# Pacing the modulation rows of a fused adaLN block, with the low-rank loads moved behind them and another scheduling model

## The chip, the cores and the metric

The kernel runs on one core of a Trainium2 chip. The metric is the device time of one execution in microseconds (us); lower is better. Five engines work side by side, each with its own in-order instruction queue: TensorE (PE) for matrix products, with its weight loads shown apart as PEld; VectorE (DVE); ScalarE (ACT); GpSimd (POOL); and SyncE (SP), which here issues nearly all DMAs.

## What is computed

One transformer-like block on x of shape (4, 1024, 2048) in float32. Six modulation vectors per batch come from one product with a 100 MB weight; a long convolution (an S4 kernel of 2048 taps) runs along the last axis; then comes a 2048 x 2048 linear layer with a low-rank update from 16 experts.

```python
mod = (_silu(L0_c) @ L0_wmod).reshape(L0_c.shape[0], 6, 1, -1)
sa, ca, ga, sb, cb, gb = (mod[:, 0], mod[:, 1], mod[:, 2], mod[:, 3], mod[:, 4], mod[:, 5])
ga = (2 * (ga >= 0) - 1) * jnp.maximum(jnp.abs(ga), 0.25)
gb = (2 * (gb >= 0) - 1) * jnp.maximum(jnp.abs(gb), 0.25)
h = _layernorm(x, axis=-1) * (1 + ca) + sa
x = x + ga * _L0_attn_ref(h, ...)      # y = irfft(rfft(h) * rfft(K)); y + D * h
h = _layernorm(x, axis=-1) * (1 + cb) + sb
x = x + gb * _L0_ffn_ref(h, ...)       # h W^T + bias + sum_e w_e (h A_e^T) Bf_e^T
```

## The kernel before

The 4096 rows of x are 32 blocks of 128 rows. For each block the kernel takes the layer-norm statistics (`stats`, L535), normalizes on DVE (`normalize`, L552), transposes 16 pieces on PE (L573), scales and shifts them on ACT (L577) and splits them into high and low float16 halves (L587, L588). The convolution is then a Toeplitz product on PE (`conv_mm`, L608): 108 matmuls a block, in three families, 41,472 columns in all. `conv_post` stores the result and takes the second layer-norm's sums (L654). The linear layer follows for 16 units of 256 rows (`ffn_unit`, L744), 5376 matmuls in all.

**Modulation rows.** `wmod` is loaded in 96 pieces of 128 x 2048 floats (1 MiB each, `mod_load`, L312), 16 for each of the six vectors. I call a piece a row. A row costs PE four matmuls (`mod_mm`, L317). The 16 rows of a vector are a `section`, which accumulates in one PSUM bank and ends in a small chain that makes a column or a gate. Section 1 (scale ca) comes first, then 0 (shift sa), then 2 (gate ga), and 4, 3, 5 later. Rows land in two pools: `wmp` with three buffers and `wms` with two, which closes after section 0.

**Early blocks.** Blocks 0, 1 and 2 are multiplied before the gate is known (`early`). For 0 and 1 the shift is missing as well; `shift_conv` and `shift_add` put it in afterwards. In this kernel one row is taken at each of the 9 `tick` calls of an early block's `conv_mm`. When section 2 is done, `gate_tile` (L668, L669) spreads the gate over 128 partitions, `conv_late` (L644, L645) applies it to the three waiting blocks, `conv_post` finishes them, and only then are the buffers of x free for blocks 4, 5 and 6.

**The low-rank part.** `prep_lora` loads A (`la`, L427) and Bf (`lb`, L440), squares, scales and splits them on ACT and DVE (L432 to L457). `merge` then adds the low-rank product to W, in eight steps of 48 matmuls each (L481). These steps, with sections 4, 3 and 5 between them, are the generator `fill`, which is advanced by `step()` during the `conv_mm` of later blocks, from block `R0` = 3 on.

**Order.** The program text gives priorities; a list scheduler in the tile framework decides the order of instructions on every engine's queue from them and from a time model of its own. The order is fixed before the run. On the chip each queue is worked off strictly in that order. `tc.issue_after` and `tc.high_priority` bend the order around the S4 kernel's steps (`toe`, taken at the row numbers `KT`).

Of the kernel before, what the change touches and what calls it, by code (L numbers as in the profile page):

```python
# [24 lines left out]
P = 128  # L25
# [9 lines left out]
class Net:  # L35
# [197 lines left out]
    def toeplitz(self, pool):  # L233
        nc, v = self.nc, self.nc.vector
        rev = pool.tile([P, P], F32, tag="rev", name="rev")
        nc.gpsimd.memset(rev, 0.0)
        nc.gpsimd.affine_select(
            out=rev, in_=rev, compare_op=ALU.not_equal, fill=1.0, base=1 - P, pattern=[[1, P]], channel_multiplier=1
        )
        kk = pool.tile([P, 16], F32, tag="kk", name="kk")  # L240
        yield from self.s4(pool)
        v.tensor_copy(kk, self.kp)
        dt = pool.tile([1, 1], F32, tag="dt", name="dt")
        nc.scalar.dma_start(out=dt, in_=self.io["D"].unsqueeze(0))
        v.tensor_tensor(kk[0:1, 0:1], kk[0:1, 0:1], dt, ADD)
        m = pool.tile([P, 1], F32, tag="km", name="km")
        v.tensor_reduce(m, kk, AX.X, ALU.max, apply_absolute_value=True)
        s, self.kinv = self.pow2(self.cst, self.allmax(pool, m, 1, "km"), 1, "ks")
        v.tensor_scalar(kk, kk, s, None, MUL)
        kd = self.dram.tile([P + D], F32, tag="kd", name="kd")  # L250
        z = pool.tile([1, P], F32, tag="kz", name="kz")
        v.memset(z, 0.0)
        nc.scalar.dma_start(out=kd[0:P].unsqueeze(0), in_=z)
        nc.scalar.dma_start(out=kd[P:].rearrange("(a b) -> a b", b=16), in_=kk)

        kb = pool.tile([P, D], F32, tag="kb", name="kb")
        src = bass.AP(tensor=kd.tensor, offset=kd.offset + 1, ap=[[1, P], [1, D]])
        nc.scalar.dma_start(out=kb, in_=src)
        self.kb = kb
        yield  # L260
        for q in range(4):
            ps = self.acc.tile([P, 512], F32, tag="a", name="kbps")
            nc.tensor.matmul(ps, rev, kb[:, ds(512 * q, 512)], start=True, stop=True)
            (v.tensor_copy if q % 2 else nc.scalar.copy)(kb[:, ds(512 * q, 512)], ps)


        kv = kb.rearrange("p (m e t) -> p m e t", e=2, t=P)
        ev, od = kv[:, :, 0, :], kv[:, :, 1, :]
        self.kf = {}
        for f in (0, 2, 1):  # L270
            hi = self.kpool.tile([P, HC * P], F16, tag=f"kh{f}", name=f"kh{f}")
            lo = self.kpool.tile([P, HC * P], F16, tag=f"kl{f}", name=f"kl{f}")
            h3, l3 = (x.rearrange("p (m t) -> p m t", t=P) for x in (hi, lo))
            if f == 0:
                src = ev
            else:
                src = pool.tile([P, 2, 512], F32, tag="kdif", name="kdif")
                src = src.rearrange("p a (c t) -> p (a c) t", t=P)
                if f == 1:
                    v.tensor_scalar(src[:, 0:1], ev[:, 0:1], -1.0, None, MUL)  # L280
                    v.tensor_tensor(src[:, 1:], od[:, 0 : HC - 1], ev[:, 1:], SUB)
                else:
                    v.tensor_tensor(src, od, ev, SUB)
            v.tensor_copy(h3, src)
            v.tensor_tensor(l3, src, h3, SUB)  # L285
            self.kf[f] = hi, lo
        yield
# [21 lines left out]
    def mod_load(self, pool, sec, j):  # L309
        w = pool.tile([P, D], F32, tag="wm", name="wm")  # L310
        src = self.io["wmod"].rearrange("(p j) n -> p j n", j=16)
        self.nc.sync.dma_start(out=w, in_=src[:, j, ds(sec * D, D)])  # L312
        return w

    def mod_mm(self, w, j):
# [272 lines left out]
                v.tensor_tensor(lo[:, sl], src, hi[:, sl], SUB)  # L588
            yield

    def conv_mm(self, pl, hs, x, tick, early):
        nc, v = self.nc, self.nc.vector
        hc, hs = hs
        y = pl["y"].tile([P, D], F32, tag="y", name="y")
        yv = y.rearrange("p (j e t) -> p j e t", e=2, t=P)
        if not early:
            gv = self.gat.rearrange("p (j e t) -> p j e t", e=2, t=P)
        sums = pl["sm"].tile([P, 2], F32, tag="sums", name="sums")

        def family(ps, f, q, first):  # L600
            pf = ps.rearrange("p j t -> p (j t)")
            last = 4 * q + 3
            for i in range(last + 1):
                o = P * max(0, i - 4 * q)
                k0 = P * max(0, 4 * q - i)
                for x, z in ((0, 0), (0, 1), (1, 0)):
                    h = hs[x][:, i] if f == 0 else hc[x][:, 2 * i + 2 - f]
                    nc.tensor.matmul(  # L608
                        pf[:, o:512], h, self.kf[f][z][:, ds(k0, 512 - o)],
                        start=first, stop=(i == last and (x, z) == (1, 0)), skip_group_check=True,  # L610
                    )
                    first = False
                if i == 3 and q == 1:
                    tick()

        for q in range(2):
            jj = slice(4 * q, 4 * q + 4)
            pa = self.acc.tile([P, 4, P], F32, tag="a", name="ya")
            family(pa, 0, q, True)
            qs = pl["t"].tile([P, 4, P], F32, tag="qs", name="qs")  # L620
            nc.scalar.copy(qs, pa)  # L621
            tick()
            pb = self.acc.tile([P, 4, P], F32, tag="a", name="yb")
            family(pb, 2, q, True)
            v.tensor_tensor(yv[:, jj, 1, :], pb, qs, ADD)
            if not early:
                v.tensor_tensor(yv[:, jj, 1, :], yv[:, jj, 1, :], gv[:, jj, 1, :], MUL)
            tick()
            family(pa, 1, q, False)
            sl = ds(1024 * q, 1024)  # L630
            if early:
                nc.scalar.copy(yv[:, jj, 0, :], pa)
            else:
                v.tensor_tensor(yv[:, jj, 0, :], pa, gv[:, jj, 0, :], MUL)  # L634
                v.scalar_tensor_tensor(y[:, sl], y[:, sl], 1.0, x[:, sl], MUL, ADD, accum_out=sums[:, q : q + 1])  # L635
            tick()
        return y, sums
# [167 lines left out]
ACC, TPS = 5, 2  # L805
PLAN = ("PNSL", "NL", "NSL", "NTL", "SL", "SL", "SL", "SL", "FSL", "SSL")
LPLAN = ("LL", "LL", "LL", "LL", "L", "0", "")
R0 = 3
WM, WMS = 3, 2
EARLY = 3  # L810
X0 = 11
LEFT0 = 30
KT = (0, 5, 7, 11)


def STQ(nc):
# [8 lines left out]
def net(ctx: ExitStack, tc: tile.TileContext, io):  # L825
# [19 lines left out]
    def section(sec, pools):  # L845
        for q in range(16):
            if q == 0:
                k.mod_begin()
            k.mod_mm(k.mod_load(pools[q % len(pools)], sec, q), q)
            yield  # L850
        if sec == 0:
            k.sa = k.mod_column(msm, k.kpool, "sa", 0.0)
            k.hinv = k.fold_scale(msm, k.ca, k.sa, "fs1")
        elif sec == 1:
            k.ca = k.mod_column(msm, k.kpool, "ca", 1.0)
        elif sec == 2:
            k.gas, (k.gad,) = k.mod_gate(msm, "gad")
        elif sec == 4:
            k.cb = k.mod_column(msm, k.cst, "cb", 1.0)
        elif sec == 3:  # L860
            k.sb = k.mod_column(msm, k.cst, "sb", 0.0)
        else:
            _, k.gbd = k.mod_gate(msm, "gbd", io["bias"])
        yield

    def merges():
        k.prep_lora(pl["lora"], pl["mrg"])
        yield
        for c in range(HC):
            yield from k.merge(pl["lora"], pl["mrg"], c)  # L870
# [3 lines left out]
    def take(g, n):  # L874
        for _ in range(n):
            next(g, None)
# [12 lines left out]
    def prep(r, shift=True):  # L889
        return k.conv_prep(pl, r, xs[r], sts.pop(r), hs, shift)  # L890

    def load(r):
        xs[r] = k.conv_load(pl, r)

    def stats(r):
        sts[r] = k.stats(pl, xs[r], "1")
# [8 lines left out]
        n += 1  # L905
    k.early_scale(msm)
    load(1)
    sec = section(0, (wms, wmp))
    for r in range(2):
        stats(r)  # L910
        take(prep(r, False), 9)
    take(sec, 1)
    with tc.issue_after(k.last.ins), tc.high_priority():
        take(toe, 2)
    take(sec, 1)

    def row():
        take(sec, 1)

    for r in range(2):  # L920
        ys[r] = k.conv_mm(pl, hs.pop(r), xs[r], row, True)
        load(r + 2)
    take(sec, 17)
    k.shift_conv(msm)
    k.shift_add([ys[r][0] for r in range(2)])
    st.close()
# [48 lines left out]
        if r >= R0 and "w" not in pr and next(fill, 0) == 0:  # L975
            early()

    sec = section(2, (wmp,))
    for r in range(2, EARLY + 1):
        stats(r)  # L980
    take(prep(2), 9)
    ys[2] = k.conv_mm(pl, hs.pop(2), xs[2], row, True)
    nxt = prep(3)
    take(nxt, 9)
    take(sec, 17)
    k.gat = k.gate_tile(pl["g"], 0)
    ratio = k.kpool.tile([P, 1], F32, tag="rat", name="rat")
    nc.vector.tensor_tensor(ratio, k.einv, k.hs[:, 0:1], MUL)
# [5 lines left out]
    stats(EARLY + 1)  # L994
    nxt = prep(EARLY + 1)
    take(nxt, 1)
    post = None
    for r in range(EARLY, 32):
        if EARLY + 2 < r + 2 < 32:
# [129 lines left out]
```

## Time and profile before

| | us |
|---|---|
| runs, median of 3 | 2149.32 (2148.76 to 2154.0) |
| profiled execution | 2149.26 |
| its span, first to last instruction | 2147.5 |
| PE busy | 2085.0 (97%), 11144 matmuls |
| DVE busy | 1313.8 (61%) |
| ACT busy | 922.0 (43%) |
| DMA moved | 483.05 MB, 225 GB/s over the span |

Between span and run time lie 1.8 us. Busy PE is not PE at its peak: the profiler models the ends of matmuls, which overlap, so a lost nanosecond shows best as a longer distance between the starts of two neighbours. "Idle before" stands beside the instruction whose start ended the idle time, with what released it. PEclk is the granted TensorE clock as a share of full speed.

### The profile page before, as it was taken

What the parts mean: (1) busy time and instruction counts of PE and PEld (TensorE: products, weight loads), DVE (VectorE), ACT (ScalarE), POOL (GpSimd) and SP (SyncE); (2) the same over time, 40 slices, a digit from 0 to 9 for tenths busy, and PEclk for the clock granted to TensorE, in tenths of its full rate; (3) what the DMA queues carried; (4) which work ended last, traced back from release to release, by engine and by line L of the source; (5) the groups of instructions that cost most, each with busy time, mean ns of one, the idle gap of its engine ahead of it and who ended that gap; (6) DMA issues with size and microseconds to landing.
All of it is one profiled execution on the core that took longest, in us unless ns stands there. A gap on an engine that the chain in (4) does not pass through costs nothing.

```text
span 2147.5 us, 28491 instructions
## 1 busy us (share of the span) xinstructions
PE 2085.0 (97%) x11144; PEld 1028.0 (48%) x11144; DVE 1313.8 (61%) x2356; ACT 922.0 (43%) x1697; POOL 3.0 (0%) x13
## 2 busy tenths in 40 slices
PE   6998999999999999999999999999999999999999
PEld 2453445455455555554545545545444444444444
DVE  5636989988999998666566565565433323232323
ACT  1335757766677776655554454454200000000000
POOL 0000000000000000000000000000000000000000
PEclk7998999999999999999999999999999999999999
DMA  9878677767874463297465465564795545455542
GB/s 389 347 266 312 253 271 286 291 247 272 312 286 160 181 221 118 94 376 281 175 242 199 174 245 189 191 240 180 266 358 165 186 152 170 165 167 166 176 156 70
DMA packets 127142, 483.05 MB, mean 225 GB/s; under 512 B 13673, under 2 KB 13802, under 8 KB 96032
## 3 DMA queue, kind: packets, MB, share of 16 engines
q1 hardware_dynamic: 126192, 477.55, 61.1%
q10 hardware_dynamic: 816, 3.69, 0.4%
q8 instruction: 87, 1.43, 0.3%
q14 instruction: 47, 0.39, 0.0%
HBM read 325.89 MB, written 155.30 MB: 224 GB/s over the span
## 4 chain that ended last, share of the span: by engine, by line
PE 59%; DVE 6%; DMA 2%; ACT 2%; issue 1%; SPq 0%; DVEq 0%; ACTq 0%
PE fZ L744 23%; PE fY L744 15%; PE fX L744 15%; PE ya L608 3%; PE tp L694 2%; PE yb L608 1%; DVE y L635 1%; DMA xo<-x1d 1%; ACT x L654 1%; DVE wch L509 1%; DVE hc L588 1%; DVE st L535 1%; DMA w<-wcd 1%; ACT t L577 1%; DVE y L634 0%
## 5 line engine op out<-in xcount | busy, mean ns | idle before, releaser
L744 PEld LDWEIGHTS <-lf 128*128 128x128 f16 x5376 | 526.0, 98 | 620.5 <-issue 0.9
L744 PE MATMUL fZ<-w,lf 128*128 128x512 f16 x2304 | 514.1, 379 | 0.6 <-ACT p L752 0.6
L744 PE MATMUL fX<-w,lf 128*128 128x512 f16 x1536 | 342.1, 379 | 0.0
L744 PE MATMUL fY<-w,lf 128*128 128x512 f16 x1536 | 342.1, 379 | 0.0
L608 PEld LDWEIGHTS <-hc 128*128 128x128 f16 x2304 | 214.1, 98 | 208.7 <-issue 45.6
L762 DVE TENSOR_TENSOR xo<-xo,gb 128x512 f32<-128x512 f32 x128 | 87.7, 690 | 235.1 <-DMA xo<-x1d 223.6
L577 ACT ACTIVATE t<-tp,sa,ca 128x128 f32<-128x128 f32 x480 | 189.3, 474 | 20.2 <-PE tp L573 19.9
L608 PE MATMUL ya<-kh,hs 128*128 128x512 f16 (+3 forms) x768 | 195.0, 328 | 1.8 <-DVE hs L588 0.7
L608 PE MATMUL ya<-kh,hc 128*128 128x512 f16 (+3 forms) x768 | 191.7, 327 | 3.8 <-ACT qs L621 3.8
L608 PE MATMUL yb<-kh,hc 128*128 128x512 f16 (+3 forms) x768 | 190.8, 326 | 0.2
L752 ACT COPY p<-fZ 128x512 f32<-128x512 f32 x64 | 37.3, 583 | 292.6 <-PE fZ L744 275.3
L608 PEld LDWEIGHTS <-hs 128*128 128x128 f16 x1152 | 107.2, 98 | 104.2 <-issue 24.1
L696 ACT ACTIVATE gt<-tp,sb,cb 128x256 f32<-128x256 f32 x256 | 125.0, 576 | 62.5 <-PE tp L694 60.9
L752 ACT COPY p<-fX 128x512 f32<-128x512 f32 x32 | 18.8, 586 | 305.8 <-PE fX L744 227.3
L317 PE MATMUL modps<-wm,sct 128*32 128x512 f32 x768 | 119.7, 663 | 24.3 <-DMA wm<-in_wmod 16.0
L608 PE MATMUL ya<-kl,hs 128*128 128x512 f16 (+3 forms) x384 | 125.8, 328 | 0.7 <-DVE kl L285 0.7
L608 PE MATMUL ya<-kl,hc 128*128 128x512 f16 (+3 forms) x384 | 125.5, 327 | 0.0
L608 PE MATMUL yb<-kl,hc 128*128 128x512 f16 (+3 forms) x384 | 125.1, 326 | 0.0
L767 DVE TENSOR_TENSOR fin<-fX,gb 128x512 f32<-128x512 f32 x32 | 22.1, 692 | 127.3 <-PE fX L744 127.2
L481 PE MATMUL lps<-lbh,lac 128*128 128x512 f16 x256 | 87.4, 389 | 8.8 <-DVE y L634 3.3
L588 DVE TENSOR_TENSOR hc<-t,hc 128x512 f16<-128x512 f32 x128 | 87.7, 685 | 8.7 <-ACT hc L587 8.6
L573 PE MATMUL tp<-ident,n 128*128 128x128 f32 x512 | 79.2, 280 | 13.8 <-ACT t L577 9.8
(259 smaller groups left out, 2230.8 us busy)
## 6 DMA issues: line engine op xcount, KB each, us to landing
wm<-in_wmod SPq DMA_DIRECT2D x96, 1024.0 KB
lfd<-lf SPq DMA_DIRECT2D x112, 512.0 KB
lf<-lfd SPq DMA_DIRECT2D x112, 512.0 KB
x<-in_x SPq DMA_DIRECT2D x32, 1024.0 KB
x1d<-y SPq DMA_DIRECT2D x32, 1024.0 KB
x<-x1d SPq DMA_DIRECT2D x32, 1024.0 KB
xo<-x1d SPq DMA_DIRECT2D x128, 256.0 KB
out<-xo SPq DMA_DIRECT2D x128, 256.0 KB
```

Of the source, the lines that this page charges most:

```text
L317: self.last = self.nc.tensor.matmul(self.modps[32 * g : 32 * g + 32, :], self.sct[:, j].rearrange("p r b -> p (r b)"), w[:, ds(512 * g, 512)],
L481: nc.tensor.matmul(ps, la[:, x, k, h], y[:, k, osl], start=(n == 0), stop=(n == 5))
L573: nc.tensor.transpose(tp[:, k], n[:, ds(P * (c0 + k), P)], self.ident)
L577: nc.scalar.activation(t[:, k], tp[:, k], AF.Identity, bias=self.sa[:, c, b : b + 1], scale=self.ca[:, c, b : b + 1],)
L588: v.tensor_tensor(lo[:, sl], src, hi[:, sl], SUB)
L608: nc.tensor.matmul(pf[:, o:512], h, self.kf[f][z][:, ds(k0, 512 - o)], start=first, stop=(i == last and (x, z) == (1, 0)), skip_group_chec ...
L694: nc.tensor.transpose(tp[:, c, r], xs[r][:, ds(P * (c0 + c), P)], self.ident)
L696: nc.scalar.activation(t[:, c0 + c], tp[:, c], AF.Identity, bias=self.sb[:, c0 + c, b : b + 1], scale=self.cb[:, c0 + c, b : b + 1],)
L744: nc.tensor.matmul(ps[name], lf[i][:, k, x, :], wc[i][k // 4][:, k % 4, y, :], start=(first and n == 0), stop=(n == 3 * HC - 1), skip_grou ...
L752: nc.scalar.copy(t, ps[name])
L762: v.tensor_tensor(x, x, self.gbias[:, h], ADD)
L767: v.tensor_tensor(t, cv, self.gbt[:, h], MUL)
```

## The change

1. Three DMAs of the convolution kernel's round trip through memory (`kd`, `kd`, `kb`) are issued from POOL and not from ACT.
2. The early blocks no longer take a row at each `tick`. A counter adds up the columns multiplied, and takes one row for every `ROWC` = 3700 columns. Sections 0 and 2 become one stream `rows`, which runs through blocks 0, 1 and 2.
3. x of blocks 2 and 3 is loaded before the products of blocks 0 and 1 and not after them; `issue_after(k.lastw.ins)` puts the x loads of blocks 0 to 3, and the whole of `prep_lora`, behind the row last loaded at that point. Statistics and preparation of block 2 are placed ahead of `shift_conv`; block 3's preparation is advanced within block 2's products.
4. `fill` starts at `R0` = 5 and not 3, with one `next(fill)` (which is `prep_lora`) before the loop over blocks.
5. `KT` moves from (0, 5, 7, 11) to (0, 5, 6, 10).
6. The scheduler runs with `schedule_with_timeline_sim=True`: another time model, and so another order on all engines.

No arithmetic is added or removed.

```diff
-        nc.scalar.dma_start(out=kd[0:P].unsqueeze(0), in_=z)
-        nc.scalar.dma_start(out=kd[P:].rearrange("(a b) -> a b", b=16), in_=kk)
+        nc.gpsimd.dma_start(out=kd[0:P].unsqueeze(0), in_=z)
+        nc.gpsimd.dma_start(out=kd[P:].rearrange("(a b) -> a b", b=16), in_=kk)
...
-        nc.scalar.dma_start(out=kb, in_=src)
+        nc.gpsimd.dma_start(out=kb, in_=src)
...
-        self.nc.sync.dma_start(out=w, in_=src[:, j, ds(sec * D, D)])
+        self.lastw = self.nc.sync.dma_start(out=w, in_=src[:, j, ds(sec * D, D)])
...
-    def conv_mm(self, pl, hs, x, tick, early):
+    def conv_mm(self, pl, hs, x, tick, early, pace=lambda n: None):
...
                 if i == 3 and q == 1:
                     tick()
+                pace(3 * (512 - o))
...
-R0 = 3
+R0 = 5
...
+ROWC = 3700
...
-KT = (0, 5, 7, 11)
+KT = (0, 5, 6, 10)
...
-        k.prep_lora(pl["lora"], pl["mrg"])
+        with tc.issue_after(k.lastw.ins):
+            k.prep_lora(pl["lora"], pl["mrg"])
...
     def load(r):
-        xs[r] = k.conv_load(pl, r)
+        if r < 4:
+            with tc.issue_after(k.lastw.ins):
+                xs[r] = k.conv_load(pl, r)
+        else:
+            xs[r] = k.conv_load(pl, r)
...
-    sec = section(0, (wms, wmp))
+    rows = (x for sec, w in ((0, (wms, wmp)), (2, (wmp,))) for x in section(sec, w))
...
-    def row():
-        take(sec, 1)
+    cols = [0]
+
+    def pace(n):
+
+        cols[0] += n
+        while cols[0] >= ROWC:
+            cols[0] -= ROWC
+            take(rows, 1)

     for r in range(2):
-        ys[r] = k.conv_mm(pl, hs.pop(r), xs[r], row, True)
         load(r + 2)
-    take(sec, 17)
+        ys[r] = k.conv_mm(pl, hs.pop(r), xs[r], lambda: None, True, pace)
+    stats(2)
+    take(prep(2), 9)
     k.shift_conv(msm)
...
-    sec = section(2, (wmp,))
-    for r in range(2, EARLY + 1):
-        stats(r)
-    take(prep(2), 9)
-    ys[2] = k.conv_mm(pl, hs.pop(2), xs[2], row, True)
+    stats(3)
     nxt = prep(3)
+    ys[2] = k.conv_mm(pl, hs.pop(2), xs[2], lambda: take(nxt, 1), True, pace)
     take(nxt, 9)
-    take(sec, 17)
+    take(rows, 40)
...
     take(nxt, 1)
+    next(fill)
     post = None
...
-    with tile.TileContext(nc) as tc:
+    with tile.TileContext(nc, schedule_with_timeline_sim=True) as tc:
```

More of the change, by code (lines that the diff above doesn't have):

```diff
@@ L911, in net @@
         take(prep(r, False), 9)
-    take(sec, 1)
+    take(rows, 1)
     with tc.issue_after(k.last.ins), tc.high_priority():
         take(toe, 2)
-    take(sec, 1)
-    def row():
-        take(sec, 1)
+    take(rows, 1)
+    cols = [0]
[3 more added lines that the diff above has]
+            cols[0] -= ROWC
+            take(rows, 1)
     for r in range(2):
-        ys[r] = k.conv_mm(pl, hs.pop(r), xs[r], row, True)
         load(r + 2)
-    take(sec, 17)
+        ys[r] = k.conv_mm(pl, hs.pop(r), xs[r], lambda: None, True, pace)
+    stats(2)
+    take(prep(2), 9)
     k.shift_conv(msm)
```

## The prediction, made before the changed kernel ran

> **What bounds the kernel now.** I read the page first, then busy time by stage, because 97% PE is an average over stages that differ.
>
> ```profile
> core 0: us, PE busy (x) PEld busy (x) DVE busy (x) ACT busy (x) POOL busy (x), PEclk, DMA share, GB/s
> 0.00:66.00 66.00, 45.22 (x213) 17.12 (x214) 40.23 (x140) 13.67 (x34) 1.84 (x10) 0.79 0.96 389
> 66.00:121.00 55.00, 54.33 (x345) 23.51 (x344) 28.27 (x63) 13.67 (x37) 0.41 (x1) 1.00 0.82 313
> 121.00:184.00 63.00, 56.41 (x374) 26.96 (x372) 22.54 (x51) 37.90 (x74) 0.35 (x1) 0.94 0.81 304
> 184.00:227.00 43.00, 34.63 (x152) 14.18 (x152) 37.20 (x72) 14.28 (x22) 0.00 (x0) 0.81 0.81 305
> 227.00:290.00 63.00, 58.30 (x345) 29.24 (x343) 59.80 (x127) 47.30 (x101) 0.00 (x0) 0.97 0.66 243
> 290.00:640.00 350.00, 345.07 (x2141) 178.20 (x2139) 314.88 (x647) 240.90 (x498) 0.00 (x0) 1.00 0.75 278
> 640.00:800.00 160.00, 150.66 (x925) 84.00 (x924) 148.88 (x319) 119.88 (x247) 0.41 (x1) 1.00 0.54 200
> 960.00:2147.00 1187.00, 1181.49 (x5692) 563.19 (x5690) 547.87 (x710) 333.82 (x479) 0.00 (x0) 1.00 0.56 197
> ```
>
> The linear layer from 960 us on is closed: its chain shows 24 matmuls in 5.18 us, 216 ns each, one after the other. All that can move lies before. To see where, I sum the PE work that stands ahead of an instruction in the built order (216, 162, 109 and 56 ns for 512, 384, 256 and 128 float16 columns, from start to start in the timeline; 0.5 us for four transposes, 1.05 for a row) and take it from the actual start. This lag is the time PE has lost so far: 34.5 us at 118 us, 38.6 at 153, 44 at 179, 62 at 228, 71 at 287, 89 at 924. So the start costs 34, the gate rows (121 to 184) 9, the passage from the last gate row to block 4 (184 to 227) 18, all later blocks 27. The passage, on DVE:
>
> ```profile
> 183.66 0.69 DVE L342 COPY mg<-modps 128x512 f32<-128x512 f32 x1 [3.73 <-PE modps L317]
> 185.68 2.29 DVE L457 TENSOR_TENSOR lbl<-lb,lbh 128x2048 f16<-128x2048 f32 x1 [1.32 <-ACT lbh L456]
> 188.69 2.29 DVE L457 TENSOR_TENSOR lbl<-lb,lbh 128x2048 f16<-128x2048 f32 x1
> ...
> 195.47 1.67 DVE L669 TENSOR_SCALAR gat<-gps,fs_i,ks_i 128x512 f32<-128x512 f32 x2 [3.90 <-PE gps L668]
> ...
> 214.10 0.69 DVE L535 BATCH_NORM_STATS2 st<-x 128x6 f32<-128x512 f32 x1
> ...
> 222.04 1.33 DVE L552 TENSOR_SCALAR n<-x,mv,rs 128x2048 f32<-128x2048 f32 x1
> ```
>
> Gate, `conv_late`, load of x 4, statistics, n: 40 us in a row. PE covers half of it with block 3 and the first L481 products. And the load of A, in SP's timeline and in DMA by stretch:
>
> ```profile
> 113.36 1.43 SPq L425 DMA_DIRECT2D lws<-in_coeffs  x2
> 114.84 1.24 SPq L425 DMA_DIRECT2D lws<-in_scales  x2
> 116.12 0.45 SPq L427 DMA_DIRECT2D la<-in_A  x1
> 120.00:124.00 4.00, 4.00 (x37) 3.58 (x34) 0.00 (x0) 0.59 (x1) 0.00 (x0) 1.00 0.61 224
> 124.00:128.00 4.00, 4.00 (x17) 2.34 (x17) 0.17 (x1) 0.00 (x0) 0.00 (x0) 0.62 0.63 237
> ```
>
> A's 2 MiB run alone at 230 GB/s against 389 for rows: it takes until about 131, 14 us, under block 1's products, where nobody waits.
>
> **The skill.** The Trainium skill, "DMA: Bandwidth & Descriptors", "Anatomy of one DMA", gives a fixed cost of about 2 us a DMA plus bytes at 436 GB/s. The trace agrees: rows that PE awaits come 2.48 us apart (starts 18.49 and 20.97), 423 GB/s. The same section says that a wait is served on the issuing sequencer before dispatch, so what stands behind it in SP's order waits too; here the row behind A was issued at 130.57 only, its predecessor at 112.94. "TensorE: Matmul & The Clock Gate", Part 1, says that the clock drops by half when PE idles for a window of 3.4 us; the 0.81 of 184 to 227 agrees.
>
> **The change, part by part.**
>
> *POOL's DMAs (1).* They take about 1 us of issue and waits from ACT, which is idle there (13.67 of 66 us). POOL's next work, the all-reduce for the early scale, is at 55.05; kb was issued at 50.44. Price 0. If POOL is 2 us slower, the transposes that now stand before kb's use cover it.
>
> *Start (3, 5, 6).* Through the last row of section 1, SP's new order has x 1 and 0.25 MiB of bias ahead of it: 1.25 MiB more, +3.1 us. The first row of section 0 stands behind x 2 too: 4.25 MiB after a row that PE took at 49.8, plus 1 MiB of kb beside it, so 62 to 63 (before: 56.3). In PE's new order block 0's last two transpose groups, all of block 1's, two more row pairs and the four kb products follow that row and precede the convolution: 64.9 for block 0, 67.8 for the next rows, block 1 until 75.5 (a group per 2 us of ACT), kb products until 79, kl 4.2 us later as before (64.4 to 68.65). The products start at about 83, with 8.2 us more work done than at 68.65. Lag 41 against 34: **+7**. Between +3 and +9, by whether ACT keeps up.
>
> *Pace (2).* 3700 columns are 1.54 us at 216 ns per 512, plus 1.05 for the row: 2.6 us, close to the 2.48 of a load. In the new PE order 16 rows of section 2 stand in 49 us of work, 3.3 us each, and SP no longer pauses from 113 to 130. The 48th row stands behind 128 us of work (before: 136). I price the waits around block 2's preparation at 5 us, as before (lag 34.6 to 38.6 there), and save the 5 that the old order lost from 153 to 179. Last gate row done: 129 + 41 + 5 = 175 us, against 183.6. In lag: 46 against 44.
>
> *Passage to block 4 (3, 4, 6).* Here is the price. Call the end of the last gate row Z. A is issued behind that row and four small loads, at Z - 6, and takes 14 to 16 us: Z + 9. ACT's new order squares it (2 x 1.95 and sums, 4.1), then three other pieces (2.5), then the root: Z + 16. On DVE the four small steps on that root stand *ahead* of the first gate piece, so the gate waits 9 us for A. Then in DVE's order: gate 4 x 0.83, 12 x 1.22 of `conv_late`, 6 x 0.35 + 0.7 of low-rank pieces: 21, Z + 37. ACT's three squares (2.2 each) beside block 3's 7 us on DVE, and small steps: Z + 47. Block 3's square, lb (3.9), lbh (3.7): Z + 57; lbl on DVE 2 x 2.29 behind its halves, Z + 60; statistics of blocks 4, 5 and 6, which all stand before n of block 4: 12 x 0.67, root and small steps 3, n 1.3: Z + 72. First products of block 4 at Z + 75. The PE work from Z to there is 35 us (block 3, eight rows of section 4, transposes), so PE loses **40**; before it lost 18 to 20. With A already there at Z + 2 it is 33, with small steps and the cold clock worse it is 44. The eight rows do not help: the 4th stands in SP's queue behind the store of y 0, which waits for `conv_late`. Lag at block 4: 41 + 5 + 40 = 86 against 62, **+24**, less 4 for sitting beside work that the old lag counts later (low-rank preparation is finished, blocks 5 and 6 have their statistics): +20.
>
> *Later blocks (4, 6).* The old order lost 27 more: 4.6 on one row at 278 with 2.5 of cold clock, 5 by 640, 13 from 640 to 924, mostly where no merge is left and a block has 17.5 us of DVE against 19.4 of PE. In the new order merges last two blocks longer, and the order of the first merges of step two still has W's load behind rows in SP's queue. I take 8 back, between 0 and 15. The linear layer's start mixes units 0 and 1 in a new way; the trace shows no wait there, so 0 to +3; I take +1.
>
> Sum: +20 - 8 + 1 = **+13** on the profiled 2149.26 (span 2147.5 plus 1.8), which lies on the median. Rounded down for the start's lower end: **2161**.
>
> **Rivals.** *Slower by the passage (0.55):* 2161, own range 2152 to 2173. *Faster (0.2):* the gate rows are done 8 us earlier, DMA works through 113 to 130, and if A lands before the gate's chain needs it, the passage costs the old 20 and not 40; with 12 won later: 2149 + 2 - 12 = 2139. It speaks for it that the 40 us chain is the same in both; against it that four steps on A stand ahead of the gate on DVE. *No change (0.15):* the new model's order wins as much in 227 to 924 (up to 20 of 27) as the passage loses: 2150. *Worse (0.1):* queues blocked by rows and stores in the later blocks as well: 2178. The side turns where the passage loses PE less than about 27 us.
>
> **Numbers.** Changes under 0.3% (6.4 us) can't be told from none here. Faster: 0.15 of the second case and 0.05 of the third, 0.2. Same: 0.05 of the second, 0.05 of the third and 0.07 of the first, 0.17. Slower: the rest of the first, 0.48, 0.05 of the third and the fourth, 0.63. The range 2137 to 2175 leaves half of the second case and most of the fourth outside.
>
> **What would show it.** Products of L608 start in earnest at about 83 us (right) or before 72 (start wrong). Row 48 ends near 175. DVE idles before the first L54 or L670 after it, released by ACT's root: the step on A. Block 4's first transposes come 65 to 75 us after row 48; under 50, the forecast is wrong. The linear layer begins at about 941 and not 928.

## The result, and the profile after

| | before | changed |
|---|---|---|
| runs, median of 5 each, on one chip | 2151.23 us (2148.76 to 2154.0) | 2163.73 us (2158.38 to 2165.91) |
| ratio | | 1.0052, interval 1.004 to 1.0065 |
| profiled execution | 2149.26 | 2165.91, the slowest of its five |
| its span | 2147.5 | 2164.1 |

The change makes the kernel 0.5% slower; 2161 was forecast. By the medians that is 12.5 us; the two profiled executions lie 16.6 us apart, since the changed kernel's was the slowest of its five. Busy time by stage, for the same stretches as before (columns as there):

```profile
core 0: us, PE busy (x) PEld busy (x) DVE busy (x) ACT busy (x) POOL busy (x), PEclk, DMA share, GB/s
0.00:66.00 66.00, 41.84 (x196) 13.60 (x196) 39.78 (x144) 9.44 (x22) 3.99 (x13) 0.76 0.98 396
66.00:121.00 55.00, 50.96 (x314) 22.29 (x311) 27.10 (x47) 17.61 (x48) 0.00 (x0) 0.95 0.76 297
121.00:184.00 63.00, 61.42 (x415) 30.23 (x412) 23.38 (x53) 21.92 (x55) 0.42 (x1) 0.97 0.79 287
184.00:227.00 43.00, 26.05 (x138) 10.22 (x138) 30.17 (x75) 30.12 (x36) 0.36 (x1) 0.78 0.71 276
227.00:290.00 63.00, 52.03 (x307) 29.61 (x308) 52.67 (x115) 34.59 (x89) 0.00 (x0) 0.85 0.52 212
...
640.00:800.00 160.00, 155.80 (x934) 83.17 (x933) 142.28 (x302) 110.80 (x223) 0.00 (x0) 0.99 0.56 207
...
960.00:2147.00 1187.00, 1187.00 (x5724) 567.40 (x5723) 544.53 (x706) 340.28 (x489) 0.00 (x0) 1.00 0.57 203
```

PE's busy column says where it went. The gate rows (121 to 184) are better, 61.4 us busy against 56.4. The passage (184 to 227) is worse, 26.1 against 34.6, and so is the stretch behind it, 52.0 against 58.3. The start is worse by 3.4, and the stretch after it (66 to 121) by 3.4 again. The granted clock was 0.78 in the passage, little under the 0.81 of before, and 0.85 behind it against 0.97.

The same passage on DVE:

```profile
177.94 0.16 DVE L436 TENSOR_TENSOR lwt<-lws 128x2 f32<-128x2 f32 x1 [6.04 <-DMA lws<-in_scales]
...
188.71 0.17 DVE L52 TENSOR_SCALAR lsa_i<-lam 128x2 f32<-128x2 f32 x1 [4.63 <-ACT lam L433]
...
208.29 0.08 DVE L646 DVE_READ_ACCUMULATOR y<-y,x 128x1 f32 x1
...
225.49 4.50 DVE L457 TENSOR_TENSOR lbl<-lb,lbh 128x2048 f16<-128x2048 f32 x2 [0.98 <-ACT lbh L456]
229.90 4.84 DVE L535 BATCH_NORM_STATS2 st<-x 128x6 f32<-128x512 f32 x8
...
238.52 1.33 DVE L552 TENSOR_SCALAR n<-x,mv,rs 128x2048 f32<-128x2048 f32 x1
```

The last gate row ended at 176.3. Both low-rank steps that stand ahead of the gate make DVE wait: 6.0 us for the four small loads of `lws`, 4.6 us for the root of A (`lam`). `conv_late` ends at 208.4, lbl stands ahead of block 4's statistics, and n comes 62 us after the row. SP's timeline there:

```profile
169.53 0.46 SPq L427 DMA_DIRECT2D la<-in_A  x1
...
206.11 0.33 SPq L651 DMA_DIRECT2D x1d<-y  x1
206.53 1.34 SPq L312 DMA_DIRECT2D wm<-in_wmod  x2
207.96 0.99 SPq L651 DMA_DIRECT2D x1d<-y  x1
209.04 0.64 SPq L312 DMA_DIRECT2D wm<-in_wmod  x1
209.77 0.44 SPq L651 DMA_DIRECT2D x1d<-y  x1
210.65 4.39 SPq L557 DMA_DIRECT2D x<-in_x  x3
```

Six transfers of 1 MiB, three stores and three rows, leave in the 5 us before x of block 4. At the 423 GB/s of the rows these are 15 us. In the kernel before, one store left in the 8 us ahead of it, and block 4's statistics began 5.8 us after its issue (at 214.10):

```profile
204.87 0.33 SPq L650 DMA_DIRECT2D x1d<-y  x1
208.27 0.33 SPq L557 DMA_DIRECT2D x<-in_x  x1
```

The prediction used SP's order for the rows, but not for x 4; it decides below. PE's two longest waits from 184 to 245 us (total, times, longest):

```profile
PE modps L317 <- DMA wm<-in_wmod: 24.6, 4, 10.8
PE tp L573 <- DVE n L552: 3.1, 1, 3.1
```

The rows named here are what PE had left to do, not what was missing: with the rows moved away it stands idle there all the same (both holds, below).

In lag, read as in the prediction at four points (the 40th product of block 0, the last gate row, a product of block 4, the last product of the convolution), and with the time of the linear layer; the last column compares what each step adds:

| | before | changed | difference of the step |
|---|---|---|---|
| start | 34.2 | 43.0 | +8.8 |
| gate rows | 46.5 | 47.6 | -7.7 |
| passage, up to block 4 | 62.3 | 81.9 | +18.5 |
| later blocks | 89.2 | 102.7 | -6.1 |
| linear layer, from its first product to the end | 1219.8 us | 1222.9 us | +3.1 |

The differences add up to 16.6 us, which is that of the two spans.

### The profile page after: what moved, and what is told of

It reads as the page before. It is cut to its first block, busy times and chain, and to the rows that moved or that the text cites. A ratio compares the mean times of both kernels' runs of the same rounds, so it can differ in the third digit from the quotient of the medians.

```text
span 2164.1 us, 28590 instructions
## 1 busy us (share of the span) xinstructions
PE 2087.2 (96%) x11144; PEld 1033.3 (48%) x11144; DVE 1301.8 (60%) x2356; ACT 927.6 (43%) x1697; POOL 6.1 (0%) x16
## 4 chain that ended last, share of the span: by engine, by line
PE 78%; DVE 9%; DMA 8%; ACT 3%; issue 1%; SPq 0%; ACTq 0%; DVEq 0%
PE fZ L745 23%; PE fY L745 15%; PE fX L745 15%; PE ya L608 10%; PE yb L608 5%; DMA wm<-in_wmod 3%; PE tp L695 3%; PE modps L317 2%; DMA x<-in_x 2%; PE lps L481 2%; PE tp L573 2%; DVE st L535 1%; DVE wch L509 1%; ACT t L577 1%; ACT x L655 1%
## 5 line engine op out<-in xcount | busy, mean ns | idle before, releaser
L763 DVE TENSOR_TENSOR xo<-xo,gb 128x512 f32<-128x512 f32 x128 | 87.9, 690 | 392.4 <-DMA xo<-x1d 378.9
L577 ACT ACTIVATE t<-tp,sa,ca 128x128 f32<-128x128 f32 x480 | 181.0, 472 | 38.2 <-PE tp L573 27.3
L317 PE MATMUL modps<-wm,sct 128*32 128x512 f32 x768 | 127.4, 711 | 50.7 <-DMA wm<-in_wmod 50.7
L535 DVE BATCH_NORM_STATS2 st<-x 128x6 f32<-128x512 f32 x128 | 79.3, 679 | 18.6 <-DMA x<-in_x 18.6
```

The source lines that it names most:

```text
L317: self.last = self.nc.tensor.matmul(self.modps[32 * g : 32 * g + 32, :], self.sct[:, j].rearrange("p r b -> p (r b)"), w[:, ds(512 * g, 512)],
L535: v.bn_stats(st[:, q], x[:, ds(512 * q, 512)])
L577: nc.scalar.activation(t[:, k], tp[:, k], AF.Identity, bias=self.sa[:, c, b : b + 1], scale=self.ca[:, c, b : b + 1],)
L763: v.tensor_tensor(x, x, self.gbias[:, h], ADD)
```

## The experiments

Theory 1 is the prediction's: the loss is the passage, and comes from where the built order puts the low-rank steps. Against it stood that the source edits cost the time under any model (2), that the pacing and the early loads do (3), or that the new model makes a worse order of any source (2b). Line numbers in the profiles of experiments are those of each one's own source. "To block 4" is the time from the end of the last gate row to block 4's first transposes.

**The two halves of the change.** Only the model put back, and only the model changed:

```diff
-    with tile.TileContext(nc, schedule_with_timeline_sim=True) as tc:
+    with tile.TileContext(nc) as tc:
```

> The changed kernel with its five edits of the source kept and the scheduler's time model put back to the old one. In its DVE order the gate stands ahead of the steps on A's root, and lbl behind n of block 4. Theory 1 (the loss is the passage from the last gate row to block 4, and it comes from the order of low-rank steps there): block 4's first transposes within 50 us of the last gate row (changed kernel: 63.7), time 2138 to 2152. Theory 2 (the edits of the source cost the time whatever the model, since A is loaded only behind the last gate row): 60 us or more from that row to block 4, time 2158 to 2168. Theory 3 (pacing and the early x loads cost at the start): products of block 0 start in earnest at 83 us or later as in the changed kernel, and the time stays above 2156.

Measured: 2150.16, ratio 0.9992 (0.9985 to 0.9998). Block 4 comes 39.6 us after the last gate row, and products start at 68 us. DVE there, from the gate's sum to block 4's statistics:

```profile
174.47 0.69 DVE L342 COPY mg<-modps 128x512 f32<-128x512 f32 x1 [8.22 <-PE modps L317]
...
205.62 0.68 DVE L535 BATCH_NORM_STATS2 st<-x 128x6 f32<-128x512 f32 x1
```

The same kernel's PE:

```profile
213.97 1.97 PE L573 MATMUL tp<-ident,n 128*128 128x128 f32 x8 [12.27 <-DVE lsb_i L54]
...
225.11 1.11 PE L573 MATMUL tp<-ident,n 128*128 128x128 f32 x4 [6.45 <-ACT t L577]
```

ACT's work before the second wait ended:

```profile
216.19 3.88 ACT L455 ACTIVATE lb<-lb,lsb_s 128x2048 f32<-128x2048 f32 x2
219.98 3.68 ACT L456 CAST lbh<-lb 128x2048 f16<-128x2048 f32 x2
```

Theories 2 and 3 fall. But the kernel gains only 2 us on the one before, though its gate rows are done 9 us earlier. The chain to block 4 is as long as before (39.9). Up to block 4's first transposes the lag grows by 16 us, before by 14: there, 24 of the first merge's 48 matmuls, about 5 us, stood between, since A and Bf were there; here A comes behind the gate rows, the first merge at 251.8, and PE idles 12.3 us. The difference comes behind the first transposes: from there to block 4's products the lag grows by 13 us, before by 1. PE waits 6.5 us there for ACT, which scales and splits Bf from 216.2 to 223.7 ahead of block 4's pieces, and its clock is 0.50 from 208 to 232. So the pacing's 5 us in the rows (lag 41.2 against 46.5) are given back, most of it behind low-rank work on ACT; the kernel with `R0` = 4 below, which has this work behind block 4, loses 5 us there and not 13.

> The kernel before with nothing but the new time model. A is loaded in the shadow of block 1 there. Theory 1: the passage stays at about 40 us from last gate row to block 4's transposes, time 2143 to 2156. Theory 2b (the new model itself makes the worse order, since it thinks loads faster than they are): time 2158 to 2170, with waits of 4 us and more of DVE or PE for loads in 66 to 230 us.

Measured: 2155.46, ratio 1.0012 (1.0004 to 1.002); to block 4 55.9 us, last gate row only at 199.2. The time lies in theory 1's range, but the passage is not the 40 us that theory 1 asked for, and DVE's wait of 6.3 us for `lws` is of the kind that 2b named. SP's first issues:

```profile
1.17 2.95 SPq L312 DMA_DIRECT2D wm<-in_wmod  x5
6.65 4.04 SPq L557 DMA_DIRECT2D x<-in_x  x4
```

The new model sends four x loads, 4 MiB, ahead of the sixth row; the start's lag is 42.3 and the rows' 62.1. It wins 22 us of this back in the later blocks, where it loses 5 us against 26.9 before. Neither half alone costs more than 0.12%, both together cost 0.52%: they meet badly.

**A freed, or later.** First, `prep_lora` without `issue_after`; then, in a kernel of its own, no `next(fill)` ahead of the loop:

```diff
-        with tc.issue_after(k.lastw.ins):
-            k.prep_lora(pl["lora"], pl["mrg"])
+        k.prep_lora(pl["lora"], pl["mrg"])
```

> The changed kernel with prep_lora no longer held behind the last gate row (the other edits and the new model kept); its steps on A and lbl then stand before or within the gate in DVE's order, with A in SBUF long before. Theory 1: no wait of DVE for A's root, block 4's transposes within 52 us of the last gate row (changed kernel: 63.7), that row up to 6 us later as A's 2 MiB now come before it; time 2146 to 2156. Theory 2 (it is the start and later blocks): 2160 to 2167.

Measured: 2171.15, 1.0085 (1.0071 to 1.0098), to block 4 62.9 us: above the ranges of both theories. DVE doesn't wait for A, and the passage is no shorter. SP's timeline:

```profile
175.22 33.49 SPq L312 DMA_DIRECT2D wm<-in_wmod  x7
208.81 0.85 SPq L473 DMA_DIRECT2D we<-in_WT  x2
211.74 2.82 SPq L312 DMA_DIRECT2D wm<-in_wmod  x2
214.62 0.90 SPq L651 DMA_DIRECT2D x1d<-y  x2
216.75 0.33 SPq L312 DMA_DIRECT2D wm<-in_wmod  x1
217.13 0.43 SPq L651 DMA_DIRECT2D x1d<-y  x1
218.48 4.69 SPq L557 DMA_DIRECT2D x<-in_x  x3
```

DVE's first statistics of block 4:

```profile
239.59 2.47 DVE L535 BATCH_NORM_STATS2 st<-x 128x6 f32<-128x512 f32 x4 [0.76 <-DMA x<-in_x]
```

Rows of section 4 and the first W, which nobody needs yet, are ahead of x 4, which lands 21 us after its issue; DMA runs at 384 to 426 GB/s from 208 on. The last gate row, now behind A and Bf, is 10 us later as well. Theory 1 is half wrong: it is the order, but not A's wait alone.

```diff
-    next(fill)
     post = None
```

> The changed kernel without the one step of fill ahead of the loop: low-rank preparation gets the priority of block 5. A is still behind the last gate row, and the order still has lbl ahead of block 4's statistics, while A's first step on DVE stands between the gate pieces. Theory 1a (the wait for A in front of the gate is the larger part): block 4's transposes 55 to 58 us after the last gate row, time 2154 to 2159. Theory 1b (lbl ahead of the statistics is the larger part): 61 to 66 us, time 2160 to 2167.

Measured: 2157.35, 1.0026 (1.0015 to 1.0037); to block 4 64.8. The passage is 1b's, as lbl still starts at 225.4. The time is below 1b's range and within that of 1a, whose passage it doesn't have; the traces differ in the later blocks (14 us lost against 21).

**Taking the passage apart.** Three holds, alone and together, on the changed kernel: DVE's small steps on A queued behind the last step of `conv_late` (`lastl`); lbl behind n of block 4 (`lastn`); section 4's rows behind the loads of x 4 and x 5 (`x5`). `issue_after` only orders a queue, and adds no wait.

```diff
+        with self.tc.issue_after(self.lastl.ins):
+            sa, ia = self.pow2(pool, am, 2, "lsa")
...
+            with self.tc.issue_after(self.lastn.ins):
+                v.tensor_tensor(self.bl[:, k], b[:, k], self.bh[:, k], SUB)
...
+        if sec == 4:
+            with self.tc.issue_after(self.x5.ins):
+                self.nc.sync.dma_start(out=w, in_=src[:, j, ds(sec * D, D)])
```

> The changed kernel with DVE's small steps on A's root (lsa, lwt) queued behind the last step of conv_late; new model kept. Theory A (the gate's wait for A is the price of the passage, as the prediction has it): DVE's waits of 6.0 us for lws and 4.6 us for A's root go from the gate's path, conv_late ends 8 to 9 us earlier (about 200 us instead of 208.4), block 4's transposes come 55 to 58 us after the last gate row instead of 63.7, time 2154 to 2159. Theory B (the low-rank chain up to lbl, which stands ahead of n of block 4, is last): conv_late ends just as early, but lbl ends at 230 us or later as before, block 4 does not gain, time 2161 to 2168.

Measured: 2157.95, 1.0028 (1.0015 to 1.004); to block 4 59.3. DVE's timeline:

```profile
201.78 0.08 DVE L647 DVE_READ_ACCUMULATOR y<-y,x 128x1 f32 x1
201.78 0.17 DVE L52 TENSOR_SCALAR lsa_i<-lam 128x2 f32<-128x2 f32 x1
...
220.79 2.46 DVE L536 BATCH_NORM_STATS2 st<-x 128x6 f32<-128x512 f32 x4
...
226.62 2.29 DVE L458 TENSOR_TENSOR lbl<-lb,lbh 128x2048 f16<-128x2048 f32 x1 [0.21 <-ACT lbh L457]
```

`conv_late` ends 6.5 us earlier, block 4 comes 4 us earlier: the waits for `lws` and A were real, and two thirds of what they cost `conv_late` reach block 4. The result lies between A and B.

> The changed kernel with lbl alone queued behind n of block 4 on DVE. Theory B: statistics of block 4 start when x 4 has landed, at 215 to 220 us instead of 229.9; block 4's transposes come 48 to 53 us after the last gate row, time 2148 to 2154. Theory C (x 4 is late itself, since its load stands behind three rows of section 4 and three stores in the memory queues, 6 MiB, 15 us at 420 GB/s): statistics start at 224 to 227 us, released by the load of x, block 4 at 57 to 60 us, time 2156 to 2161.

Measured: 2159.87, 1.003 (1.0016 to 1.0044); to block 4 61.7. DVE's timeline:

```profile
226.93 2.47 DVE L536 BATCH_NORM_STATS2 st<-x 128x6 f32<-128x512 f32 x4 [2.53 <-DMA x<-in_x]
...
236.42 4.49 DVE L458 TENSOR_TENSOR lbl<-lb,lbh 128x2048 f16<-128x2048 f32 x2
```

The mechanism is theory C's: with lbl away the load of x stands there; it landed 16 us after its issue at 210.55. Statistics begin only 3 us sooner than with lbl in front, and block 4 gains 2.

> The changed kernel with lbl behind n of block 4, and in addition the rows of section 4 queued on SP behind the loads of x 4 and x 5. Theory C: x 4 lands at about 216 to 218 us, block 4's transposes come 45 to 50 us after the last gate row, 8 us or more ahead of the kernel with lbl moved alone, time 2145 to 2152. Theory B without C: no difference to the kernel with lbl moved alone.

Measured: 2152.85, 1.0003 (0.9995 to 1.0012); to block 4 50.4, 11 us less than with lbl moved alone; time and step lie just above C's ranges. SP's timeline:

```profile
206.62 3.20 SPq L656 DMA_DIRECT2D x1d<-y  x3
211.75 2.32 SPq L562 DMA_DIRECT2D x<-in_x  x2
214.16 1.64 SPq L314 DMA_DIRECT2D wm<-in_wmod  x3
```

DVE's first statistics of block 4:

```profile
219.12 2.47 DVE L540 BATCH_NORM_STATS2 st<-x 128x6 f32<-128x512 f32 x4 [1.02 <-DMA x<-in_x]
```

C is shown: with lbl moved in both kernels, moving the rows too makes x 4 land earlier and the time shorter, on intervals that lie apart. The two holds, of which neither adds or removes work, take back by the medians 10.9 of the 12.5 us that the change cost. The traces show 6.5 of these up to block 4 (lag 81.9 to 75.4); the other 4 lie in the later blocks, where one trace doesn't settle so little (POOL's DMAs, below). The hold of the rows alone was not run: that it would gain nothing as long as lbl, done at 230.0, stands in front is argued and not shown. x 4 still has three stores ahead of it and lands 7.4 us after its issue. Rows are no cover any more: of the seven that stood ahead of block 4 in PE's order one is left, so block 4 gains 13 us and the lag half of that. PE stands idle from 208 to 224 (0.01 us busy), and its clock falls to 0.50, as the Trainium skill says of a PE that is idle for a window of about 3.4 us ("TensorE: Matmul & The Clock Gate", Part 1).

> The changed kernel with all three: gate free of A, lbl behind n of block 4, section 4's rows behind x 4 and x 5. If the three costs add up in one chain: conv_late ends at about 200 us, x 4 lands at 208 to 210, block 4's transposes 36 to 42 us after the last gate row, lag there about 60 us, time 2138 to 2147. If another wait takes their place, named by what releases block 4's n: 2148 or more.

Measured: 2153.18, 1.0009 (1.0002 to 1.0016); to block 4 49.6. The gains don't add. The profiled execution was the slowest of 22 (2160.03), so its trace shows where time can go, and not what the median lost. `conv_late` ends at 206.5 in this order, x 4 leaves at 208.9, statistics begin at 217.57 after 2.32 us of waiting for x, so the loads and stores stand there, and from block 4's first transposes to its products the lag rises by 11 us more (71.3 to 82.2): ACT scales and splits Bf between block 4's pieces there (227.1 to 237.4), and PE waits 3.7, 2.3 and 1.5 us for it.

**Another place for the low-rank step.** Old model, `R0` = 3, and `next(fill)` right where the pools open, before block 2; then the same source under the new model:

```diff
-R0 = 5
+R0 = 3
...
     fill = rest()
+    next(fill)
...
-    next(fill)
     post = None
...
-    with tile.TileContext(nc, schedule_with_timeline_sim=True) as tc:
+    with tile.TileContext(nc) as tc:
```

> The changed kernel with the old time model, fill from block 3 on as before, and the one step of it (prep_lora) moved up to where its pools open, ahead of block 2's products; pacing, x loads and POOL's DMAs kept. A and Bf then load among the paced rows, where DMA has some 15 us free, and 26 us of merge and rows stand between the last gate row and block 4 in PE's order. Theory D (the source edits are good but for the place of prep_lora: held behind the gate rows it takes away PE's cover and puts 4 MiB in front of x 4): last gate row done at 174 to 180 us, block 4's transposes 38 to 42 us after it with PE idle under 14 us of these, lag there about 55, time 2139 to 2147. Theory E (pacing itself costs, or A among the rows delays the gate rows as much as it gains): last gate row at 183 us or later, time 2149 to 2156.

Measured: 2150.59, 0.9984 (0.9976 to 0.9992), the best of all ratios. To block 4 43.6, but the last gate row ends at 182.5: nearly E's number for the row, and a time in E's range. DVE's order there:

```profile
186.84 4.49 DVE L457 TENSOR_TENSOR lbl<-lb,lbh 128x2048 f16<-128x2048 f32 x2 [4.43 <-ACT lbh L456]
192.19 0.68 DVE L342 COPY mg<-modps 128x512 f32<-128x512 f32 x1
```

With A and Bf among them the rows end 8 us later than with the model alone put back, and DVE picks the gate's sum up 9.7 us after the last row, because lbl and its wait for ACT stand in front. From the row to block 4's products PE loses 18 us, against 30 with the model alone put back (lag at block 4 67.0 against 70.9): merge stands there again, and ACT's low-rank work no longer stands between block 4's pieces. The two were not taken apart here. The profiled execution took 2154.40, 3.8 us above the median.

> The same source under the new time model. Theory D alone: the start costs 6 us more than under the old model (products of block 0 in earnest at 81 to 84 us), and the passage is as good, time 2146 to 2152. Theory F (the new model's order puts what is ready by its fast loads ahead of what the chip needs, whatever the source): block 4's transposes 50 us or more after the last gate row, time 2155 to 2166.

Measured: 2170.94, 1.008 (1.0066 to 1.0094); to block 4 65.2, lag there 74.7. The passage is F's; the time is above F's range, for 33 us are lost in the later blocks. Which step of the order does that wasn't followed up.

> The changed kernel with the old time model, no step of fill ahead of the loop and fill from block 4 on: A, Bf and the low-rank steps come behind block 4's statistics, n and transposed pieces on DVE and ACT. Pacing, x loads and POOL's DMAs kept. Theory G (with the gate rows done at 174 us, what is left of the passage under the old model is the 40 us chain of gate, conv_late, x 4 and n; the low-rank casts on ACT cost 6.5 us more there, which go): last gate row at 173 to 176 us, block 4's transposes 38 to 41 us after it with no gap over 3 us inside them, lag behind them about 64 instead of 70.7, time 2142 to 2147. Rival (the first merge then comes too late and PE waits for its operands in block 5, giving it back): 2148 to 2153.

This one is the old model, no `next(fill)` ahead of the loop, `R0` = 4. Measured: 2158.57, 1.0034 (1.0022 to 1.0046). The passage is as theory G has it (37.9 us, gaps of at most 2.3 us within the transposes, lag 62.6 at block 4). Then the rival comes, and stronger than its number: PE waits for block 5's pieces, rows and the first merge, the lag is 77 by 256 us, and 36 us are lost from block 4 to the end of the convolution.

**POOL's DMAs**, all three put back on ACT:

```diff
...
-        nc.gpsimd.dma_start(out=kb, in_=src)
+        nc.scalar.dma_start(out=kb, in_=src)
```

> The changed kernel with the three DMAs of the convolution kernel's round trip issued from ACT again. Prediction's price 0: within 3 us of the changed kernel, 2160 to 2167. Rival: POOL's own issue delays kb, which then lands at about 60 instead of 62.6 us and lets products start 2 us or more earlier: 2156 to 2161.

Measured: 2159.89, 1.003 (1.0018 to 1.0042), 3.8 us under the changed kernel, on intervals that touch. PE's and SP's orders are the same in both kernels. The time lies in the rival's range, but the rival's cause isn't seen: POOL issued kb at 53.2, ACT at 56.4. The start's lag is 41.7 against 43.0, which is 1.3 us: the eight products of kb took 3.6 us here and 5.3 in the changed kernel, where the clock was 0.69 from 76 to 80 us and not 1.00. The other 4 in the traces lie in the later blocks, where the same order lost 15 and 21 us; I take that for scatter between executions. For the single steps above (2157.35, 2157.95, 2159.87) it means that a gain in time over the changed kernel isn't shown, only the earlier block 4 of the two holds among them; both holds together (at most 1.0012) are clear of this kernel too (at least 1.0018).

The runs together, times of the last gate row and of the step to block 4 in us:

| kernel | ratio | last gate row | to block 4 | lag: start | rows | block 4 | end |
|---|---|---|---|---|---|---|---|
| before | 1 | 183.6 | 39.9 | 34.2 | 46.5 | 62.3 | 89.2 |
| changed | 1.0052 | 176.3 | 63.6 | 43.0 | 47.6 | 81.9 | 102.7 |
| old model, all edits | 0.9992 | 174.4 | 39.6 | 35.8 | 41.2 | 70.9 | 91.0 |
| new model, no edit | 1.0012 | 199.2 | 55.9 | 42.3 | 62.1 | 87.9 | 92.9 |
| A freed | 1.0085 | 186.3 | 62.9 | 41.0 | 46.2 | 86.4 | 106.4 |
| lbl and rows held | 1.0003 | 177.1 | 50.4 | 43.9 | 48.5 | 75.4 | 91.9 |
| old model, low-rank step early | 0.9984 | 182.5 | 43.6 | 35.4 | 49.1 | 67.0 | 94.2 |

## Why the prediction was right, and where it was not

- *POOL's DMAs, 0*: 1.3 us at the start, which go with a lower clock there and not with a later kb; more isn't shown.
- *Start, +7*: +8.8. Products came in earnest at 82.7, forecast 83. The reason is the new model's order: with the old one and all edits the start's lag is 35.8, with the new one and no edit 42.3.
- *Pace*: last gate row at 176.3, forecast 175; lag 47.6, forecast 46.
- *Passage, PE loses 40*: 34.3. The +20 of the sum is the lag at block 4, start and rows included; it rose by 19.6 (62.3 to 81.9). The total held, its terms only in part. Block 4 came 63.6 us after the row, just under the forecast's 65 to 75, because the chain ran about 5 us ahead of the forecast from A on: A's root was there after 12.4 us (forecast 16), `conv_late` ended after 32 (37), lbl after 53.7 (60), and statistics to transposes took 10 (12). Ahead of the gate DVE waited 4.6 us for A's root (forecast 9) and 6.0 for `lws`, which the forecast didn't name as a wait. The step that failed without harm to the number is the one that leaves out the bytes ahead of x 4: the statistics were made to wait for lbl alone, and "With A already there at Z + 2 it is 33" made A's arrival decide. With A there PE lost 40 (A freed, 46.2 to 86.4); with lbl moved alone block 4 gained 2 us, with lbl and the rows 13. That the number stood is luck: behind 6 MiB of rows and stores x 4 landed at 226.9 (the kernel with lbl moved, whose SP queue issued x 4 and what is ahead of it at the same times to about 0.1 us), 3 us before lbl ended at 230.0.
- *Later blocks, -8*: -6.1 in the profiled execution, but the same order gave -12 in another (POOL's DMAs put back), so the size isn't settled.
- *Linear layer, 0 to +3*: it began at 941.2 (forecast 941) and was 3.1 us longer; PE's longest wait there is 2.7 us for the transformed W.
- *Rivals*: the faster case rested on A landing early enough. The run with A freed shows that this alone makes it worse: the gate rows end 10 us later, and x 4 lands later still. The case of no change asked for up to 20 us won in the later blocks; 6 to 12 were won.
- *A DMA's cost*: the section that the prediction names gives 2 us plus bytes at 436 GB/s for DMAs issued from GpSimd; the rows are issued from SP, and the trace shows the rate alone (423 GB/s). No term of the sum uses the 2 us.

What was wrong in the frame: the passage was put down to edits 3, 4 and 6 as one thing. Edits without the model and the model without edits each stay within 0.12%; the cost is what the new model made of these edits, which only the built order shows.

## What to carry to other kernels

When gated work ends sooner, look at what else stands on the path behind it, for that may have moved too: with the old model, 9 us won on the gate rows were spent in front of block 4's products. Count the bytes issued ahead of a load, not only the instructions ahead of its user. Two causes that end within 3 us of each other hide each other: lbl moved alone brought block 4 2 us, lbl and the rows 13. And judge an edit together with the scheduler's model: each half was near neutral, both were 0.5% slower.

## What was unexpected of the hardware

The four loads of 4-byte pieces (`lws`, 1.4 us of issue for two) made DVE wait 6.0 us, until 177.94, 8.4 us after the last was issued, with rows and A in flight beside them. With the model put back it was 8.5 us (issued by 168.15, used at 176.68 after 1.5 us of waiting). And the same orders on PE and SP lost 15 and 21 us in the later blocks in two executions of nearly equal kernels, so that a difference of a few us there can't be read from one trace.
